# Sums, copies and one PSUM bank moved in a two-level seven-product kernel on one core

## The chip, the cores and the metric

The kernel runs on one core of one Trainium2 chip. Times are device microseconds of that core, from runs of the whole program. A profile is one more execution, taken by the hardware profiler; the span in it runs from the first to the last instruction.

The engines are named as the profile names them: PE (matmul; PEld is its weight load), DVE (vector), ACT (scalar), POOL (GpSimd), and SP, which here only issues DMAs. Each takes its instructions in the order in which the program lists them.

## What is computed

A conditioned block over x of 32 sequences x 128 tokens x 512 features, all in float32. Cut to what matters:

```python
emb = silu(t) @ ada_w + ada_b                       # shift, scale, gate per sequence
norm = where(m, layernorm(x) * (1 + scale) + shift, 0)
fwd = gelu(norm @ ssm_w1 + b1) @ ssm_w2 + b2        # bwd: the same with other weights
x = x + gate * where(m, fwd + bwd, 0)
ff_ada = silu(t) @ ffada_w + ffada_b
ff_norm = layernorm(x) * (1 + scale_mlp) + shift_mlp
h = gelu_tanh(ff_norm @ ff_w1 + ff_b1)              # 512 -> 1024
out = x + gate_mlp * (h @ ff_w2 + ff_b2)            # 1024 -> 512
```

The first half touches masked tokens only (the mask marks the tails of the sequences), the second half touches all 4096 tokens.

## The kernel before

**First half, to about 88 us.** Masked tokens are gathered into 512 slots, four tiles of 128 (s0 to s3). For each pair of tiles `hidden` (L182) forms gelu(xT w1) and `project` (L196) multiplies it with w2 into one PSUM bank `po`; bias, gate and x are then added on DVE and the rows stored to a DRAM tile, `x1_rows`. For the last tile, s3, these three steps are `with_bias`, `with_gate` and `with_x` (L1173 to L1182), and `with_x(3)` is also what issues the last store of `x1_rows`, on SP's queue. Between the matmuls of s3's `project` four transposes make xT of the second group of sequences.

**Second half.** The 32 sequences are done in four pairs of groups (`p` = 0 to 3, eight sequences a pair, four a group). A pair goes through two products:

*FirstProduct* (h = gelu(x w1)). The blocks of x and of w1 are multiplied with a scheme of seven products in place of eight, on two levels. The outer level gives seven *streams*, done in the order 1, 2, 5, 6, 3, 7, 4 (`STREAMS`); inside a stream the inner level gives seven *products*, P1 to P7. One product of one stream is a *phase* (`phase`, L896): two matmul instructions of 128x256 float32, four records in the trace. In what follows P6(1) is product P6 of stream 1. A stream has two PSUM accumulators, `e` (from the pool ps_h) and `a` (from ps_o), three buffers each in turn. Around the phases stand the sums that make the scheme work:

- `TokenBlocks.one(j)` (L767), on DVE: the *inner* sums of x that streams 1 and 2 use (s1, s2, a21, s4); 128x1024 each. P5 reads s1, P6 reads s2, P3 reads s4.
- `token_sums(j, n)` (L824), on DVE: the *outer* sums, for streams 5, 6 (tiles sx and sy), 3 and 4 (in place), each in four parts n = 0 to 3; 128x512, the last part 128x256. Part 0 serves P5 and P6, part 1 P1 and P2, part 2 P7 and P4, part 3 P3.
- `seed(j)` (L945): puts a stream's `a` (for streams with a prior result, plus that result) into `e` before P2 adds onto it. On ACT for stream 1, on DVE for the others.
- After P6 DVE writes e = a + p5 (L930), on which P3 then adds; after P7 and P4 DVE writes a sum of `a` out of PSUM (L935, L940); P2 and P3 are copied out or put through gelu by ACT. `with_p5` (L953) adds a kept P5 to a result on POOL; the sum after P6(2) reads such a result.

Streams overlap by *windows* (L994): P5, P1 of the new stream, P3, P7 of the old one, P2, P6 of the new, P4 of the old. A dictionary `fills`, filled with `put(window, place, function)`, says what else is recorded behind which phase: token sums, the gathers that overwrite masked tokens of the next pair with rows of `x1_rows` (`take_first_half`, on POOL's queue), and layernorm statistics.

*SecondProduct* (out = h w2). One level of the same scheme: P1 to P7, each for two halves of the tokens, U and V, 14 steps (`ORDER`) of eight matmul instructions. `first_block` and `second_block` (L1036, L1046) make its sums s1 and, in place, s2 on DVE; `keep_and_seed` (L795) copies `e` to a tile p5 and `a` to `e`, on ACT. P5V reads the second half of s1, which is made of gelus of the end of the first product (quarter "21" of stream 4).

The first three steps of the second product stand between the last phases of the first one (L1288 to L1307), and the next pair's stream 1 between its last steps (L1341 to L1352). For the next pair, x is normalised and transposed in 32x32 blocks on DVE, turned by 28 small DMAs on SP's queue and 4 on ACT's, and scaled on ACT.

Everything is recorded under a manual schedule: on each engine the instructions run in the order in which these functions are called. So the order of the calls is the order of the work. The SP queue at the opening of pair 0 holds, in this order: two loads of weight sums (tw, 896 KB each, `load_weights`), the store of `with_x(3)`, four loads of the next pair's x (512 KB each), and much later the next weight sums.

Of the kernel before, what the change touches and what calls it, by code (L numbers as in the profile page):

```python
# [9 lines left out]
F32 = mybir.dt.float32  # L10
# [12 lines left out]
def kernel(  # L23
# [51 lines left out]
    P = 128  # L75
# [21 lines left out]
    ps_h = ctx.enter_context(tc.tile_pool(name="ps_h", bufs=3, space=bass.MemoryType.PSUM))  # L97
    ps_o = ctx.enter_context(tc.tile_pool(name="ps_o", bufs=3, space=bass.MemoryType.PSUM))
# [45 lines left out]
    w2 = ssm.tile([P, HC, D], F32, name="w2")  # L144
# [48 lines left out]
            h.append(t)  # L193
        return h

    def project(i, h, w, name, between=None):  # L196

        po = ps_o.tile([P, 512], F32, tag="o", name=f"po_{name}_{i}")
        for f in range(HC):
            if between and f in between:  # L200
                between[f]()
            nc.tensor.matmul(po, h[f][:, ts(i, P)], w[:, f, :], start=(f == 0), stop=(f == HC - 1))  # L202
        return po
# [272 lines left out]
    for key, vec in (("ssm1", ssm_b1), ("bwd1", bwd_b1), ("ff1", ff_b1)):  # L476
        n = vec.shape[0] // P
# [133 lines left out]
    h1 = []  # L611
# [46 lines left out]
    of_x = {}  # L658
# [133 lines left out]
    def bank_of(product, unit):  # L792
        return unit[1] if product in ("P1", "P6", "P7", "P4") else unit[0]

    def keep_and_seed(unit, name):  # L795

        e, a = unit
        p5 = gp.tile([P, 512], F32, tag="p5", name=f"p5_{name}", bufs=3)
        nc.scalar.copy(p5, e)
        nc.scalar.copy(e, a)  # L800
        return p5
# [211 lines left out]
    class SecondProduct:  # L1013
# [29 lines left out]
                ALU.add,  # L1043
            )

        def second_block(self, c):  # L1046

            nc.vector.tensor_tensor(
                self.s1[c], self.s1[c], self.ha[:, : HC // 2, self.cols[c]], ALU.subtract
            )  # L1050
# [22 lines left out]
        def step(self, step, late=False):  # L1073
            p, ha, hb, s1, w = self.p, self.ha, self.hb, self.s1, fw2_of.of
            hh = HC // 2
            product, n = ORDER[step][:2], ORDER[step][2]
            c = "UV".index(n)
            tok = self.cols[c]
            e, a = self.banks[c]
            bank = bank_of(product, (e, a))  # L1080
            src = {
                "P1": ha[:, :hh, tok], "P2": ha[:, hh:, tok], "P3": ha[:, hh:, tok],
                "P4": hb[:, hh:, tok], "P5": s1[c], "P6": s1[c], "P7": hb[:, :hh, tok],
            }[product]
            last = p == NP - 1 and step == len(ORDER) - 1
            for i in range(2):
                part = bank[:, ts(i, D // 2)]
                if last:
                    part = ps_t.tile([P, 512], F32, tag="tr", name=f"last_{i}")[:, : D // 2]
                for k in range(hh):  # L1090
                    nc.tensor.matmul(  # L1091
                        part,
                        src[:, k, ts(i, P)],
                        w[product][:, k, :],
                        start=(last and k == 0),
                        stop=True,
                        skip_group_check=True,
                    )
                if last:

                    t = tp.tile([P, D // 2], F32, tag="t", name=f"t_last_{i}")
                    gate = self.gate[1][:, 2 * c + i, : D // 2]
                    nc.vector.tensor_tensor(t, part, gate, ALU.mult)
                    xt = self.xs[1][c][:, i, : D // 2]
                    nc.vector.tensor_tensor(xt, xt, t, ALU.add)
                    nc.sync.dma_start(out[(2 * p + 1) * G + 2 * c + i, :, : D // 2], xt)
            if product == "P5":
                self.p5[c] = keep_and_seed((e, a), f"o{p}_{c}")
                if not late:
                    self.second_block(c)  # L1110
            elif product == "P2":
                self.finish(c, 0, 0, e)

                nc.vector.tensor_tensor(ha[:, hh:, tok], ha[:, hh:, tok], s1[c], ALU.subtract)
            elif product == "P6":
                nc.vector.tensor_tensor(e, a, self.p5[c], ALU.add)
            elif product == "P3":
                self.finish(c, 0, 1, e)
                self.store(c, 0)
            elif product == "P7":  # L1120
                t = tp.tile([P, 512], F32, tag="t", name=f"c22_o{p}_{c}")
                nc.vector.tensor_tensor(t, a, self.p5[c], ALU.add)
                self.finish(c, 1, 1, t)
                if p == NP - 1 and n == "V":
                    b = (2 * p + 1) * G + 2 * c
                    nc.sync.dma_start(
                        out[b : b + 2, :, D // 2 :].rearrange("b s d -> s b d"),
                        self.xs[1][c][:, :, D // 2 :],
                    )
                    self.finish(c, 1, 0, a)  # L1130
            elif product == "P4" and not last:
                self.finish(c, 1, 0, a)
                self.store(c, 1)
# [20 lines left out]
    h1 = hidden(xT_t, NH, w1, 0, AF.Gelu, "s1", ssm)  # L1154
# [13 lines left out]
    def turn(k):  # L1168
        return lambda: transposed(1, xn_b, xT[1], k)
# [10 lines left out]
    def with_x(at):  # L1180
        nc.vector.tensor_tensor(tail[at], tail[at], xc[at], ALU.add)
        nc.sync.dma_start(x1_rows[ts(at, P), :], tail[at])  # L1182
# [3 lines left out]
    def keep_and_turn():  # L1186
# [2 lines left out]
        with_gate(2, gs[0])  # L1189
        with_x(2)  # L1190

    po = project(1, h1, w2, "s3", {0: turn(0), 1: turn(1), 2: keep_and_turn, 4: turn(3)})

    store_weight_sums(4, 2)
    of_x[0] = TokenBlocks(0, xT)
# [6 lines left out]
    now = FirstProduct(0, of_x[0].cut(), of_w)  # L1202
    for j in (1, 2):
        now.load_weights(j)
    now.apart(1)
    for j in (2, 3, 4):
        of_x[0].one(j)
    now.do(1, "P1")
    now.seed(1)
    now.do(2, "P1")  # L1210
    now.do(1, "P2", "P5", "P6")
    with_x(3)
    x_of[1] = load_x(1, spare)
    now.token_sums(1, 0)
    now.do(2, "P5")
    now.do(1, "P7")
    now.with_p5(2, "22")
    now.seed(2)
    now.token_sums(1, 1)
    now.do(1, "P3")  # L1220
    now.with_p5(2, "12")
# [8 lines left out]
    for p in range(NP):  # L1230
# [4 lines left out]
        def put(w, n, f, *args):  # L1235
            fills.setdefault(w, {}).setdefault(n, []).append(lambda: f(*args))

        if p:
            put(1, 1, now.token_sums, 2, 2)
            put(1, 3, now.token_sums, 2, 3)  # L1240
        for n, at in enumerate(((1, 4), (1, 6), (1, 6), (2, 1)) if p else ((2, 1), (2, 1), (2, 3), (2, 3))):
            put(*at, now.token_sums, 3, n)
        for n, at in enumerate(((2, 3), (2, 4), (2, 6), (2, 6)) if p else ((2, 4), (2, 4), (2, 6), (2, 6))):
            put(*at, now.token_sums, 4, n)
        put(3, 6, now.load_weights, 3)
        put(4, 6, now.load_weights, 4)
        second = SecondProduct(p, now.h, xs)
# [56 lines left out]
            to_feature_rows(0, nc.sync)  # L1304
        second.load_gate(1)
        second.first_block(1, 0, 2)
        second.second_block(0)  # L1307
        fill = {5: [lambda: second.third_block(0)], 7: [lambda: second.third_block(1)]}

        def put(step, f, *args):  # L1310
# [5 lines left out]
        if more_pairs:  # L1316

            for i in range(G):
                put(2 + i // 2, blocks, 1, i)
            for k in range(KC):  # L1320
                put(4 + k // 2, lambda k: scaled(2 * (p + 1), xT[0], k), k)
                put(7 + k // 2, lambda k: scaled(2 * (p + 1) + 1, xT[1], k), k)
                if k == 1:
                    put(4, to_feature_rows, 1, nc.sync, nc.sync, nc.sync, nc.scalar)

            def begin(j):
                if j == 1:
                    of_x[p + 1] = TokenBlocks(p + 1, (xT[0], xT[1]))
                of_x[p + 1].one(j)

            put(8, begin, 1)
            put(9, begin, 2)
            put(9, begin, 3)
            put(10, begin, 4)

            def next_product():
                nxt["p"] = FirstProduct(p + 1, of_x[p + 1].cut(), of_w)
                nxt["p"].load_weights(1)

            nxt = {}  # L1340
            put(10, next_product)  # L1341
            put(11, lambda: nxt["p"].do(1, "P5", "P1"))
            for n in range(4):
                put(11 + n // 2, lambda n: nxt["p"].token_sums(1, n), n)
            for n in range(2):
                put(13, lambda n: nxt["p"].token_sums(2, n), n)
            if p + 2 < NP:
                x_of[p + 2] = [[], []]
                put(11, lambda: x_of[p + 2][0].extend(load_side(p + 2, 0)))
                put(13, lambda: x_of[p + 2][1].extend(load_side(p + 2, 1)))  # L1350
            put(12, lambda: nxt["p"].do(1, "P2", "P6"))
            put(13, lambda: nxt["p"].load_weights(2))  # L1352
# [4 lines left out]
        if more_pairs:  # L1357
            now = nxt["p"]
# [11 lines left out]
    with tc.If(more > 0):  # L1370
# [11 lines left out]
        with tc.For_i(0, more, 1):  # L1382
# [12 lines left out]
            for half_no, (mod, was, wbs, bias, bcol, func) in enumerate(  # L1395
# [7 lines left out]
                for j, w in enumerate(was):  # L1403
                    n = FF // len(was)
                    nc.sync.dma_start(wa[:, :, ts(j, n)], w.rearrange("(k p) f -> p k f", p=P))
                for j, w in enumerate(wbs):
                    n = HC // len(wbs)
# [69 lines left out]
```

## Time and profile before

| | us |
|---|---|
| median of 3 runs | 466.88 |
| the runs | 464.16, 466.93, 466.88 |
| the profiled execution | 463.4 |
| its span | 461.7 |

The granted clock of PE was 0.998 of full speed over the span. By stretches of the span (busy us of each engine, then the mean busy share of the DMA engines):

| stretch, us | what runs | PE | DVE | ACT | POOL | DMA |
|---|---|---|---|---|---|---|
| 0 to 58 | first half, slots 0 to 255 | 51.90 | 37.91 | 11.61 | 11.86 | 0.95 |
| 58 to 88 | first half, slots 256 to 511 | 30.00 | 24.54 | 11.06 | 13.23 | 0.43 |
| 88 to 111 | pair 0, first product, opening | 21.84 | 22.83 | 11.08 | 10.51 | 0.74 |
| 111 to 144 | pair 0, first product, rest | 32.94 | 24.09 | 17.19 | 25.61 | 0.31 |
| 144 to 175 | pair 0, second product | 30.90 | 21.83 | 13.79 | 0.00 | 0.53 |
| 175 to 199 | change to pair 1 | 23.47 | 22.95 | 7.71 | 7.52 | 0.68 |
| 199 to 267 | pair 1 | 67.84 | 48.36 | 33.29 | 28.17 | 0.40 |
| 267 to 358 | pair 2 | 90.84 | 68.60 | 41.02 | 36.15 | 0.48 |
| 358 to 462 | pair 3 | 98.91 | 61.03 | 28.48 | 24.79 | 0.26 |

How to read it: a busy PE is not PE at its peak, since ends of matmuls are modelled; whether PE lost time is seen from the distance between starts. Two instructions of an engine can overlap by some hundredths of a us in a timeline, for the same reason. A timeline merges like instructions that follow each other (x2 is two), and gives the idle time ahead of one only from 0.15 us or so on. The name of a tile leaves its buffer's number out, so that `e_m` is the accumulator e of any stream.

### The profile page before, as it was taken

To read this page: it belongs to the slowest core of one execution; us is meant where nothing else is said; L and a number is where in the kernel's file an instruction comes from. 1 tells how busy PE (TensorE), PEld (TensorE's weight loads), DVE (VectorE), ACT (ScalarE), POOL (GpSimd) and SP (SyncE) were. 2 spreads that over 40 slices of the span, in tenths; PEclk is the share of its full clock that TensorE was granted. 3 is DMA by queue.
4 is the path that set the end of the run, shared out by engine and by line. 5 is a ranking of instruction groups with operands and counts; after the bars stand their busy time and mean duration, and the time that the engine had idled before them with its cause. 6 is when DMAs were issued, how large, how long until landed. Compare 5 with 4: busy or idle time off the path is not lost.

```text
span 461.7 us, 5825 instructions
## 1 busy us (share of the span) xinstructions
PE 448.6 (97%) x2000; PEld 364.2 (79%) x2000; DVE 332.1 (72%) x538; ACT 175.2 (38%) x380; POOL 157.8 (34%) x153
## 2 busy tenths in 40 slices
PE   6899999999999999999999999999999999999995
PEld 2385385677888888788888888888888888888884
DVE  4649868999678839986787498867873995434645
ACT  3121021744445361344455513444455144562000
POOL 6210083048980000489700005987000025660000
PEclk9999999999999999999999999999999999999999
DMA  8999835692207734833077258220872342222022
GB/s 276 386 407 361 307 136 88 204 346 88 106 5 224 105 84 137 297 100 130 1 229 114 69 182 298 92 87 14 226 108 67 134 163 79 81 85 98 0 85 101
DMA packets 82418, 70.41 MB, mean 153 GB/s; under 512 B 63168, under 2 KB 63696, under 8 KB 81362
## 3 DMA queue, kind: packets, MB, share of 16 engines
q1 hardware_dynamic: 67298, 57.03, 39.4%
q0 software_dynamic: 4480, 11.66, 7.1%
q10 hardware_dynamic: 10608, 1.32, 2.0%
q8 instruction: 17, 0.28, 0.2%
q14 instruction: 15, 0.12, 0.1%
HBM read 56.83 MB, written 13.17 MB: 152 GB/s over the span
## 4 chain that ended last, share of the span: by engine, by line
PE 69%; DVE 9%; ACT 7%; POOL 5%; SPq 4%; issue 4%; DMA 1%; POOLq 0%; ACTq 0%; DVEq 0%
PE a_m L905 15%; PE a_o L1091 14%; PE e_m L905 12%; PE e_o L1091 12%; PE ph_s L188 6%; PE po_s L202 4%; SPq L744 4%; POOL hb L989 2%; ACT hb L867 2%; ACT xT L727 1%; DVE sx L834 1%; DVE xT L725 1%; ACT ha L867 1%; DVE xn_sy L838 1%; PE part_s L282 1%
## 5 line engine op out<-in xcount | busy, mean ns | idle before, releaser
L956 POOL TENSOR_TENSOR ha<-p_m,ha 128x512 f32<-128x512 f32 x20 | 26.9, 1345 | 152.5 <-ACT ha L963 143.3
L1091 PE MATMUL e_o<-fw,ha 128*128 128x256 f32 x256 | 57.9, 379 | 0.0
L727 ACT ACTIVATE xT<-xT,modT 128x128 f32<-128x128 f32 x112 | 44.1, 480 | 30.5 <-DMA xT<-xn 30.3
L1091 PE MATMUL a_o<-t,hb 128*128 128x256 f32 x240 | 54.1, 379 | 0.0
L1091 PEld LDWEIGHTS e_o<-fw,ha 128*128 128x128 f32 x256 | 48.6, 190 | 6.6
L1091 PEld LDWEIGHTS a_o<-t,hb 128*128 128x128 f32 x240 | 45.6, 190 | 6.2
L673 POOL DMA_INDIRECT x<-x_rows,slot_i x32 | 36.4, 1136 | 28.7 <-DMA x_rows<-t_s 18.1
L867 ACT ACTIVATE hb<-hb,biasT 128x256 f32<-128x256 f32 x64 | 29.0, 501 | 27.8 <-POOL hb L989 19.3
L956 POOL TENSOR_TENSOR hb<-p_m,hb 128x512 f32<-128x512 f32 x20 | 28.2, 1409 | 20.4 <-DVE hb L935 20.1
L919 ACT COPY p_m<-e_m 128x512 f32<-128x512 f32 x27 | 15.8, 585 | 49.2 <-PE e_m L905 46.8
L1091 PE MATMUL e_o<-fw,s 128*128 128x256 f32 x128 | 29.2, 381 | 0.5 <-DVE s L1039 0.3
L963 ACT COPY ha<-e_m 128x512 f32<-128x512 f32 x32 | 18.5, 578 | 28.0 <-PE e_m L905 27.7
L1091 PE MATMUL a_o<-t,s 128*128 128x256 f32 x128 | 28.9, 379 | 0.0
L1091 PE MATMUL a_o<-fw,ha 128*128 128x256 f32 x128 | 28.9, 379 | 0.0
L202 PE MATMUL po_s<-w,h_s 128*128 128x512 f32 x64 | 28.6, 593 | 0.0
L188 PE MATMUL ph_s<-xT_s,w 128*128 128x256 f32 x128 | 28.6, 382 | 0.0
L1091 PEld LDWEIGHTS e_o<-fw,s 128*128 128x128 f32 x128 | 24.1, 190 | 4.8 <-DVE s L1039 1.7
L188 PEld LDWEIGHTS ph_s<-xT_s,w 128*128 128x128 f32 x128 | 24.0, 190 | 4.7 <-ACT h_s L192 1.5
L1091 PEld LDWEIGHTS a_o<-t,s 128*128 128x128 f32 x128 | 24.3, 190 | 3.3
L1091 PEld LDWEIGHTS a_o<-fw,ha 128*128 128x128 f32 x128 | 24.3, 190 | 3.3
L867 ACT ACTIVATE ha<-e_m,biasT 128x256 f32<-128x256 f32 x48 | 20.0, 468 | 15.5 <-PE e_m L905 10.2
L930 DVE TENSOR_TENSOR e_m<-a_m,ha 128x512 f32<-128x512 f32 x20 | 13.9, 697 | 16.6 <-POOL ha L956 6.6
(210 smaller groups left out, 870.3 us busy)
## 6 DMA issues: line engine op xcount, KB each, us to landing
tw<-t_rows SPq DMA_DIRECT2D x16, 896.0 KB, 4.7
x<-in_x_dram SPq DMA_DIRECT2D x16, 512.0 KB, 8.4
gate<-gate_rows POOLq DMA_DIRECT2D x8, 1024.0 KB
out_dram<-x SPq DMA_DIRECT2D x15, 512.0 KB, 3.1
xT<-xn SPq DMA_DIRECT2D x92, 64.0 KB, 2.4
fw<-in_L_cond_ff_w_dram SPq DMA_DIRECT2D x2, 2048.0 KB
ada_f<-in_L_cond_ffada_w_dram SPq DMA_DIRECT2D x4, 768.0 KB, 13.7
ada_a<-in_L_cond_ada_w_dram SPq DMA_DIRECT2D x4, 512.0 KB, 5.9
```

What stands on the lines that cost most here:

```text
L188: nc.tensor.matmul(ph[:, :n], w[:, k, ts(f, P)], xT[:, k, :], start=(k == 0), stop=(k == KC - 1))
L202: nc.tensor.matmul(po, h[f][:, ts(i, P)], w[:, f, :], start=(f == 0), stop=(f == HC - 1))
L673: nc.gpsimd.indirect_dma_start(out=xs[i // G][i % G // 2][:, i % 2], out_offset=None, in_=x1_rows[:slots, :], in_offset=bass.IndirectOffse ...
L727: nc.scalar.activation(out, src, AF.Identity, bias=shift, scale=scale)
L744: queues[b % len(queues)].dma_start(dst[ts(q, R), b], src[ts(b, R), q])
L867: nc.scalar.activation(dst[:, n], src[:, n], AF.Gelu_apprx_tanh, bias=biasT[:, f : f + 1])
L905: nc.tensor.matmul(bank[:, ts(n, QT)], self.w_block(j, product)[:, ts(n, P)], self.x_block(j, product), start=(product in ("P1", "P5") and ...
L919: nc.scalar.copy(p5, e)
L930: nc.vector.tensor_tensor(e, a, p5, add)
L956: nc.gpsimd.tensor_tensor(self.place(RESULT[j], c), self.p5[j], other, ALU.add)
L963: nc.scalar.copy(self.place(RESULT[j], c), src)
L1091: nc.tensor.matmul(part, src[:, k, ts(i, P)], w[product][:, k, :], start=(last and k == 0), stop=True, skip_group_check=True,)
```

## The change

Nothing is computed otherwise; the same instructions run, with the same sizes. What moves:

1. *Bank.* `project` can be told from which PSUM pool its bank comes; the last tile, s3, takes one of ps_h in place of ps_o.
2. *Opening of pair 0, on DVE.* Before: s2, a21, s4, then the sum after P6(1), `with_x(3)`, sx part 0, the sum after P7(1), the seed of stream 2, sx parts 1 to 3, the sum after P6(2). After: s2, a21, the sum after P6(1), s4, the seed of stream 2, the sum after P7(1), sx part 0, `with_x(3)`, sx parts 1 to 3, the sum after P6(2). PE's order is as it was. The order on POOL and SP is as it was too, but the store of `with_x(3)` and the x loads behind it on SP follow a DVE instruction that now stands later.
3. *Windows of pairs 1 to 3, on DVE.* Before: sy parts 0 and 1, the seed of stream 2, sy part 2, the sum after P7(1), sy part 3, the first part of stream 3's sum, the sum after P6(2), then the other parts. After: sy part 0, the seed of stream 2, the sum after P7(1), sy parts 1 and 2, the sum after P6(2), sy part 3 and stream 3's sum, whose last part stands behind the sum after P7(2).
4. *Second product, on ACT.* `keep_and_seed` of the first half (U) is called with the second block and no more right behind P5U. On ACT the order was: gelus of the end of stream 4 (two), copy to p5, copy to e, gelus (two); it becomes four gelus, then the two copies. This holds in every pair.

```diff
-    def project(i, h, w, name, between=None):
+    def project(i, h, w, name, between=None, bank=(ps_o, "o")):
-        po = ps_o.tile([P, 512], F32, tag="o", name=f"po_{name}_{i}")
+        pool, tag = bank
+        po = pool.tile([P, 512], F32, tag=tag, name=f"po_{name}_{i}")
...
-        def second_block(self, c):
+        def seed_and_second_block(self, c):
+            self.p5[c] = keep_and_seed(self.banks[c], f"o{self.p}_{c}")
             nc.vector.tensor_tensor(
                 self.s1[c], self.s1[c], self.ha[:, : HC // 2, self.cols[c]], ALU.subtract
             )
...
             if product == "P5":
-                self.p5[c] = keep_and_seed((e, a), f"o{p}_{c}")
                 if not late:
-                    self.second_block(c)
+                    self.seed_and_second_block(c)
...
-    po = project(1, h1, w2, "s3", {0: turn(0), 1: turn(1), 2: keep_and_turn, 4: turn(3)})
+    between = {0: turn(0), 1: turn(1), 2: keep_and_turn, 4: turn(3)}
+    po = project(1, h1, w2, "s3", between, (ps_h, "h"))
...
-    for j in (2, 3, 4):
+    for j in (2, 3):
         of_x[0].one(j)
     now.do(1, "P1")
     now.seed(1)
     now.do(2, "P1")
     now.do(1, "P2", "P5", "P6")
+    of_x[0].one(4)
+    now.do(2, "P5")
+    now.seed(2)
+    now.do(1, "P7")
+    now.with_p5(2, "22")
+    now.token_sums(1, 0)
     with_x(3)
     x_of[1] = load_x(1, spare)
-    now.token_sums(1, 0)
-    now.do(2, "P5")
-    now.do(1, "P7")
-    now.with_p5(2, "22")
-    now.seed(2)
     now.token_sums(1, 1)
     now.do(1, "P3")
     now.with_p5(2, "12")
...
         if p:
-            put(1, 1, now.token_sums, 2, 2)
-            put(1, 3, now.token_sums, 2, 3)
-        for n, at in enumerate(((1, 4), (1, 6), (1, 6), (2, 1)) if p else ((2, 1), (2, 1), (2, 3), (2, 3))):
+            for n, at in enumerate(((1, 3), (1, 4), (1, 6))):
+                put(*at, now.token_sums, 2, 1 + n)
+        for n, at in enumerate(((1, 6), (2, 1), (2, 1), (2, 3)) if p else ((2, 1), (2, 1), (2, 3), (2, 3))):
             put(*at, now.token_sums, 3, n)
-        for n, at in enumerate(((2, 3), (2, 4), (2, 6), (2, 6)) if p else ((2, 4), (2, 4), (2, 6), (2, 6))):
+        for n, at in enumerate(((2, 4), (2, 4), (2, 6), (2, 6))):
             put(*at, now.token_sums, 4, n)
...
         second.first_block(1, 0, 2)
-        second.second_block(0)
+        second.seed_and_second_block(0)
...
-            for n in range(2):
-                put(13, lambda n: nxt["p"].token_sums(2, n), n)
+            put(13, lambda: nxt["p"].token_sums(2, 0))
```

## The prediction

> **What bounds the kernel now.** I read the page's busy shares and chain first, then the timelines of PE, DVE, POOL and ACT around the three places that the change touches. Columns of a timeline: start and length in us, engine, line, operation, tiles, then in brackets the idle time before it and what ended it. The page:
>
> ```profile
> PE 448.6 (97%) x2000; PEld 364.2 (79%) x2000; DVE 332.1 (72%) x538; ACT 175.2 (38%) x380; POOL 157.8 (34%) x153
> PE 69%; DVE 9%; ACT 7%; POOL 5%; SPq 4%; issue 4%; DMA 1%; POOLq 0%; ACTq 0%; DVEq 0%
> ```
>
> PE carries the chain. One phase (four matmul records) starts 0.86 us after the last when nothing is missing; anything over that is lost. The opening of pair 0, PE:
>
> ```profile
> 87.96 1.03 PE L905 MATMUL a_m_alone<-xT,fw 128*128 128x256 f32 x4
> 89.12 1.10 PE L905 MATMUL a_m<-xT,fw 128*128 128x256 f32 x4
> ...
> 93.84 1.13 PE L905 MATMUL a_m_alone<-xT,t 128*128 128x256 f32 x4 [0.17 <-DVE e_m L930]
> ...
> 96.36 1.13 PE L905 MATMUL e_m<-xT,fw 128*128 128x256 f32 x4 [0.53 <-DVE e_m L949]
> ...
> 104.59 1.13 PE L905 MATMUL a_m<-xT,t 128*128 128x256 f32 x4 [0.19 <-DVE hb L935]
> ```
>
> Start to start, with about 0.1 for the slower first matmuls behind a stop, I count losses of 0.37 (89.12), 0.43, 0.79, 0.45, then 0.15 and 0.40 at 107.33 and 109.47, and 0.27 each at 120.10 and 122.11. In later pairs: 0.42 at each of 144.10, 236.50 and 327.80; 0.48, 0.37 and 0.44 at 189.47, 191.57 and 198.98; 0.10, 0.08 and 0.20 at 281.54, 306 and 372.90. From 58 us to the end PE loses 6.2 us in all: no edit here can give more.
>
> But who is late? DVE and POOL at the opening:
>
> ```profile
> 91.96 1.22 DVE L774 TENSOR_TENSOR s<-xT,s 128x1024 f32<-128x1024 f32 x1
> 93.09 0.69 DVE L930 TENSOR_TENSOR e_m<-a_m_alone,p_m 128x512 f32<-128x512 f32 x1
> 93.69 0.68 DVE L1181 TENSOR_TENSOR t_s<-t_s,xc 128x512 f32<-128x512 f32 x1
> ...
> 95.62 0.69 DVE L949 TENSOR_TENSOR e_m<-a_m,ha 128x512 f32<-128x512 f32 x1
> 96.21 2.36 DVE L834 TENSOR_TENSOR sx<-xT 128x512 f32<-128x512 f32 x2
> 98.50 1.49 DVE L834 TENSOR_TENSOR sx<-s 128x256 f32<-128x256 f32 x1
> 99.91 0.69 DVE L930 TENSOR_TENSOR e_m<-a_m,ha 128x512 f32<-128x512 f32 x1
> ```
>
> ```profile
> 96.29 1.73 POOL L956 TENSOR_TENSOR hb<-p_m,hb 128x512 f32<-128x512 f32 x1 [18.78 <-DVE hb L935]
> 97.99 1.72 POOL L956 TENSOR_TENSOR ha<-p_m,ha 128x512 f32<-128x512 f32 x1
> 102.35 1.37 POOL L673 DMA_INDIRECT x<-x_rows,slot_i  x1 [2.65 <-DMA x<-in_x_dram]
> ```
>
> No DVE line from 80 to 113 us shows idle time: the opening is bound by DVE's total, not by its order. POOL has no gap from 102.35 to 127, and the waits of 120.10 and 122.11 hang on it (DVE's sum at 119.35 had waited 2.02 us for POOL). The end of the first product, ACT:
>
> ```profile
> 141.34 0.57 ACT L799 COPY p_o<-e_o 128x512 f32<-128x512 f32 x1
> 141.93 0.57 ACT L800 COPY e_o<-a_o 128x512 f32<-128x512 f32 x1
> 142.42 0.91 ACT L867 ACTIVATE hb<-hb,biasT 128x256 f32<-128x256 f32 x2
> ```
>
> **What the Trainium skill says.** "PSUM — Partial Sum Buffer", section "PSUM bank collisions raise a hardware error": accesses are guarded by bank. The trace agrees: a_m of stream 2, in po_s3's buffer, starts at 89.12 only when the bias add of 88.29 (0.68) has read it. Section "Engine vs sequencer instructions": the ACT, DVE and GpSimd queues are strict FIFO, so order alone can cost. "SBUF — State Buffer", section "Who interferes with whom": a DVE instruction with two SBUF inputs and a GpSimd one that reads SBUF lock each other out. The trace agrees: the two POOL adds take 1.73 and 1.72 us here against 1.27 at 121.94, and the DVE sums beside them (2.36 for two, 1.49 for a half one) against 0.68 and 0.41.
>
> **The change, part by part.** Units: DVE 128x512 sum 0.60 start to start, 128x1024 1.13; PE phase start to its reader 1.06 (P7(1) 93.84, less its 0.1, to DVE 95.01); DVE start to the PE phase behind it 0.75 (93.09 to 93.84).
>
> *Bank.* Stream 2's first phase no longer waits: P6(1) starts 91.41 instead of 91.78. The ring of ps_h shifts by one; its buffers' last readers were gelus before 73 us, so no new wait.
>
> *Opening order.* DVE comes to the P6(1) sum at 91.96 but PE gives it at 91.41 + 1.06 = 92.47: DVE now idles 0.51. Then sum 92.47, s4 93.07, seed 94.20, P7(1) sum 94.80, sx0 95.40, with_x, sx1 to sx3. P7(1) starts 93.22, P3(1) waits for s4 to 94.35 (before 94.81), P2(2) 95.3 (before 96.36): the 0.43 and 0.79 go. But the next sum, P6(2), stands behind the same set of DVE work. Four sums, a half one, and the two POOL adds that lock DVE for about 1.19 each: 95.40 + 2.74 + 2.38 = 100.5; before, 99.91. P3(2) needs it: about 101.2 against 100.78. So PE ends the reordering about 0.5 late; 0.54 of it is swallowed by the POOL waits at 120.10 and 122.11. Net 0 (ends: −0.4 if the locks fall on sums from PSUM, +0.8).
>
> *SP and POOL behind it.* with_x goes from 93.69 to about 97.2, its store from 94.40 to 97.9, and with it four x loads that stand behind on SP. The first gather waits for the first load's landing: 101.50 in the trace. There the loads queued behind weight loads (those end at 98.5); issued 3.5 later they find idle DMA engines: store 97.9, load 98.3, plus about 3.5 (a lone 256 KB store took 2.0; 256 packets of 2 KB pass in 1.35), so 101.9. POOL starts 0.4 late (ends 0 and 3.5) and, having no slack, hands it on: **+0.4** for pair 0.
>
> *Window order, pairs 1 to 3.* Moving one 0.60 sum (and its lock) behind the seed and the P7(1) sum frees 0.48 and 0.37 at 189 to 192, 0.10 at 281, 0.20 at 372. In pair 1 it meets the next thing: P5(6) at 198.98 starts right behind tw's last packet (198.47), whose load SP issues behind the last store and x loads. That does not move, so pair 1 gives 0; pairs 2 and 3 give **−0.3**. Sums of streams 3 and 4 shift by some slots inside windows 1 and 2 where DVE idles 0.63 at 196.29: 0 (ends −0.2, +0.5).
>
> *ACT copies.* The last two gelus can start when DVE's P4 sum is done, 140.79 + 0.65, near 141.5 instead of 142.42; DVE's s1 sum then follows its transpose, 142.56 instead of 143.35, and P5V is ready at 143.3, before its turn at 143.79. The copies, now 142.4 to 143.6, feed P2U at 147.66: covered by 3.5 us of P5V. Gone: 0.42 in pairs 0, 1 and 2. Pair 0's is hidden again: pair 1 starts on xT, whose DMAs SP issues without a break from 143.13 to 163.9, whatever PE does. Left: **−0.85** (ends 0, −1.3).
>
> Sum: 0.4 − 0.3 − 0.85 = **−0.75 us**, span 461.7 to about 460.95. The profiled execution took 463.4, 3.5 under the median of 466.88; the same step from the median is 466.1.
>
> **Rivals.** *All stops go*: if DVE kept up, everything named up to 122 except the POOL waits, the 0.48, 0.37, 0.10, 0.20, and three times 0.42: 2.6 + 1.15 + 1.26, near −4.5 with side effects, 462.4. Against it: DVE's unbroken row. *Slower*: the x loads land the full 3.5 later; POOL's chain, hence PE at 120.10, moves 3.5; +3.5 − 1.15 = +2.35, 469.2. It decides once the first gather starts later than 103.5 (102.35 + 1.15). For it: POOL waited on just this load, 2.65. Against it: the loads were held by other traffic. *Nothing shows*: DVE or DMA hides pairs 2 and 3 as well; 0, 466.9.
>
> **Numbers.** Chances: forecast 0.5, all stops 0.12, slower 0.2, nothing 0.18. A change under 1% cannot be told from none here; the three runs alone spread 0.6%. Forecast 466.1; range 463.0 to 468.2, from half of the full gain with the spread of the runs to most of the slower case. Over 1% faster needs 4.7 of the 6.2 us lost: 0.05, over 1% slower 0.03, within 1% 0.92.
>
> **What would show it.** Right: a_m of stream 2 0.86 behind the phase before; a DVE gap of 0.5 before the P6(1) sum; P3(2) no earlier than 100.7; first gather at 102.3 to 103.2; no stop at 236 and 328, but one before P5(6) of pair 1. Wrong: P3(2) near 99.7 (order counted after all), or a gather past 103.5.

## The result, and the profile after

| | before | after |
|---|---|---|
| median, us | 465.41 (21 runs, 463.07 to 467.85) | 465.20 (21 runs, 462.27 to 468.52) |
| the profiled execution | 463.4, span 461.7 | 462.27, span 460.6 |

The ratio of after to before is 1.0003, 95% interval 0.9986 to 1.0020: no change that can be measured. The two traces differ by 1.1 us, but the execution profiled of the changed kernel was the shortest of its 21 and that of the kernel before lay 2.0 under its median. So traces are used below for where a wait is, and timings for what it is worth.

The page of the changed kernel, busy shares and chain by engine:

```profile
PE 447.5 (97%) x2000; PEld 364.8 (79%) x2000; DVE 331.0 (72%) x538; ACT 175.4 (38%) x380; POOL 157.5 (34%) x153
PE 74%; DVE 10%; SPq 4%; DMA 3%; issue 3%; ACT 3%; POOL 2%; ACTq 0%; DVEq 0%; POOLq 0%
```

Busy times are the same within 0.3%. The chain lost ACT and POOL (12% before, 5% now) and gained PE and DMA (1% before, 3% now): a transfer has become a wait. From 58 us on PE loses 5.4 us of starts, 6.2 before. PE's timeline of the opening (L906 is L905 of before; lines move by one to three):

```profile
87.81 1.03 PE L906 MATMUL a_m_alone<-xT,fw 128*128 128x256 f32 x4
88.67 1.03 PE L906 MATMUL a_m<-xT,fw 128*128 128x256 f32 x4
89.80 1.13 PE L906 MATMUL e_m<-xT,fw 128*128 128x256 f32 x4
...
101.32 0.92 PE L906 MATMUL e_m<-s,fw 128*128 128x256 f32 x3 [1.24 <-DVE e_m L931]
```

P1(2) follows P1(1) after 0.86: the wait for the bank is gone. But P2(1) follows only after 1.13, and its first matmul is slow. ACT's timeline says why:

```profile
83.00 6.26 ACT L728 ACTIVATE xT<-xT,modT 128x128 f32<-128x128 f32 x16 [0.27 <-DMA xT<-xn]
89.17 0.58 ACT L952 COPY e_m<-a_m_alone 128x512 f32<-128x512 f32 x1
```

The copy that seeds `e` of stream 1 stands behind sixteen scalings of xT; P2(1) needs it. The 0.37 of the bank, with 0.1 for slow first matmuls in it, came back here. DVE's timeline, same stretch:

```profile
92.75 0.70 DVE L931 TENSOR_TENSOR e_m<-a_m_alone,p_m 128x512 f32<-128x512 f32 x1 [0.86 <-ACT p_m L920]
...
96.29 0.69 DVE L1182 TENSOR_TENSOR t_s<-t_s,xc 128x512 f32<-128x512 f32 x1
96.89 3.44 DVE L835 TENSOR_TENSOR sx<-xT 128x512 f32<-128x512 f32 x2
...
100.58 0.68 DVE L931 TENSOR_TENSOR e_m<-a_m,ha 128x512 f32<-128x512 f32 x1
```

DVE, which had no gap before, now idles 0.86 ahead of the sum after P6(1), and with_x(3) (L1182) has moved from 93.69 to 96.29. Two sums that take 0.60 each alone took 3.44: POOL's two additions ran beside them. POOL's timeline:

```profile
96.36 1.74 POOL L957 TENSOR_TENSOR hb<-p_m,hb 128x512 f32<-128x512 f32 x1 [18.91 <-DVE hb L936]
98.07 1.71 POOL L957 TENSOR_TENSOR ha<-p_m,ha 128x512 f32<-128x512 f32 x1
103.23 1.17 POOL L674 DMA_INDIRECT x<-x_rows,slot_i  x1 [3.45 <-DMA x<-in_x_dram]
```

POOL's first gather waits 3.45 for the x load that stands behind with_x(3), and starts at 103.23 (before 102.35).

Later, all three stops before P5V are gone, and those before P2(2) of pairs 1 to 3 too. In their place PE stops before P5(6) of pair 1 and of pair 2. First the kernel before, in pair 1, then the changed one:

```profile
198.98 1.10 PE L905 MATMUL e_m<-xn_sy,tw 128*128 128x256 f32 x4 [0.21 <-issue]
...
198.68 1.10 PE L906 MATMUL e_m<-xn_sy,tw 128*128 128x256 f32 x4 [0.52 <-DMA tw<-t_rows]
...
289.62 1.10 PE L906 MATMUL e_m<-xn_sy,tw 128*128 128x256 f32 x4
```

Counted as in the prediction, 0.75 is lost in pair 1 (0.44 before) and 0.30 in pair 2 (0.10 at the P2(2) of pair 2 before); pair 3 has 0.23 at 398.64, before P5(4). tw's last packets end at 198.15, 289.14 and 398.07, about half a us ahead of each of these starts: PE has caught up with its weight sums.

### The profile page after: what moved, and what is told of

It reads as the page before. It is cut to its first block, busy times and chain, and to the rows that moved or that the text cites. A ratio compares the mean times of both kernels' runs of the same rounds, so it can differ in the third digit from the quotient of the medians.

```text
span 460.6 us, 5827 instructions
## 1 busy us (share of the span) xinstructions
PE 447.5 (97%) x2000; PEld 364.8 (79%) x2000; DVE 331.0 (72%) x538; ACT 175.4 (38%) x380; POOL 157.5 (34%) x153
## 4 chain that ended last, share of the span: by engine, by line
PE 74%; DVE 10%; SPq 4%; DMA 3%; issue 3%; ACT 3%; POOL 2%; ACTq 0%; DVEq 0%; POOLq 0%
PE a_o L1093 17%; PE a_m L906 16%; PE e_o L1093 13%; PE e_m L906 12%; PE ph_s L188 6%; PE po_s L203 4%; SPq L745 4%; DMA tw<-t_rows 2%; ACT xT L728 1%; DVE sx L835 1%; DVE xT L726 1%; DVE s L775 1%; PE part_s L283 1%; PE pm_f L263 1%; PE last L1093 1%
```

## The experiments

All ratios are to the kernel before, with the 95% interval. The last two columns are from each kernel's trace, in us behind its own P1(1): the start of P3(2), and of P3(3).

| label | what | median | ratio | P3(2) | P3(3) |
|---|---|---|---|---|---|
| (before) | | 465.41 | 1 | 12.83 | 32.15 |
| (after) | parts 1 to 4 | 465.20 | 1.0003 (0.9986 to 1.0020) | 13.51 | 32.97 |
| x1_copies | before, part 4 | 464.97 | 1.0000 (0.9969 to 1.0030) | 12.83 | 33.42 |
| x2_windows | before, part 3 | 464.60 | 0.9979 (0.9962 to 0.9996) | 12.83 | 33.77 |
| x3_opening | before, parts 1 and 2 | 466.77 | 1.0033 (1.0012 to 1.0054) | 13.57 | 33.03 |
| x4_early_x | after, with_x(3) early | 463.97 | 0.9977 (0.9954 to 0.9999) | 13.28 | 32.73 |
| x5_p5_on_dve | after, two additions to DVE | 465.87 | 1.0007 (0.9990 to 1.0025) | 12.67 | 35.10 |
| x6_tw_first | after, tw ahead of x | 462.91 | 0.9959 (0.9943 to 0.9976) | 13.27 | 32.72 |
| x8_p5_first | after, P5(1) ahead of P2(1) | 462.13 (1 run) | | 13.15 | 32.61 |
| x7_best | x5, x6, x8, with_x(3) early | 463.46 | 0.9967 (0.9951 to 0.9982) | 11.76 | 34.18 |
| x9_gathers | x7, three gathers later | 462.66 | 0.9948 (0.9927 to 0.9969) | 11.75 | 32.87 |
| x10_gathers_alone | after, three gathers later | 466.03 | 1.0010 (0.9991 to 1.0029) | 13.50 | 35.04 |
| x11_gathers_pool | x9 without x5's edit | 463.20 | 0.9968 (0.9947 to 0.9990) | 12.90 | 32.70 |
| x12_old_opening | before, parts 3 and 4, tw ahead of x | 463.23 | 0.9941 (0.9917 to 0.9966) | 12.83 | 33.76 |

### The parts alone

The first four test the theory that the change is a sum of a loss in the opening and gains later, against the rival that each part is hidden by itself. The diffs of x1, x2 and x3 are the hunks of their parts in the change. x4 puts with_x(3) and the x loads directly behind the sum after P6(1):

```diff
     now.do(1, "P2", "P5", "P6")
+    with_x(3)
+    x_of[1] = load_x(1, spare)
     of_x[0].one(4)
...
-    with_x(3)
-    x_of[1] = load_x(1, spare)
     now.token_sums(1, 1)
```

x1_copies:

> The kernel before with part 4 alone (copies behind the gelus). Theory (each part is hidden in part by what is late next): the stops of about 0.42 us before P5V are gone in pairs 0, 1 and 2; pair 0's gain comes back as a longer stop at P2(2) or P4(1) of pair 1, where DVE and the turning DMAs set the time, so the stops at 189 to 192 grow from 0.85 to about 1.25; span about 0.85 shorter than before (461.7 to 460.9), ratio about 0.998. Rival (all of it reaches the end): 1.26 shorter, and no stop grows. Rival (nothing): the stops move behind another ACT wait, span unchanged.

No stop before P5V is left. In pair 3 the stop before P2(2) grew from 0.20 to 0.84. In pair 1 it grew from 0.48 to 0.89, but the 0.37 before P4(1) went, so the two together came to 0.89 and not to the 1.25 expected, and the stop before P5(6) shrank from 0.44 to 0.07. So this trace shows the theory's longer stop in pair 3 only. The timing shows nothing, in an interval of 0.3% either way.

x2_windows:

> The kernel before with part 3 alone (windows of pairs 1 to 3). Theory: the stops at P2(2) and P4(1) are gone in pairs 1 to 3 (0.85, 0.10, 0.20), but the stop before P5(6) grows in pair 1 from 0.44 to about 1.3, because the load of weight sums lands when it did; 0.3 at most is left from pairs 2 and 3; ratio 0.999 to 1.000. Rival (order counts in full): P5(6) of pair 1 starts 0.85 earlier, span about 1.15 shorter, ratio 0.9975.

The stops at P2(2) and P4(1) of pairs 1 to 3 are gone, and P5(6) of pair 1 stopped for 1.78, longer than the theory's 1.3. The timing is 0.21% better, as the rival had it, and more than that trace lets one see. One reading is that parts 3 and 4 open each other's way: P5V early is worth something only where P2(2) does not wait, and both end at tw. That is not tested; no run has these two parts alone.

x3_opening:

> The kernel before with parts 1 and 2 alone (bank and opening). Theory (DVE's total binds, and the x loads come late): P3(2) starts about 0.5 later than before (near 101.3) behind one stop of about 1.5 us, the first gather starts near 103.2 instead of 102.35, and PE leaves the stops at 120 to 122 about 0.7 to 0.8 later than before; span 0.5 to 0.8 longer unless pair 1 hides it, ratio 1.001 to 1.002. Rival (PE's order counts): the opening ends at least 0.5 earlier, ratio below 0.999.

The timing puts the cost of the opening by itself at 0.33%, some 1.5 us, with 0.12% to 0.54% in the interval. The trace repeats the marks of the changed kernel, with P2(1) late by 0.42 and P3(2) by 1.51, but does not show where 1.5 us would be lost. Its first gather came at 102.35, no later than before, but took longer with those behind it, and P3(3), at 33.03, lies among the starts that kernels with the old opening have (32.15 to 33.77).

x4_early_x:

> The changed kernel with with_x(3) and the x loads right behind the P6(1) sum, as early as before; all else as changed. Theory (POOL's chain from the first gather sets pair 0): DVE's total is the same, so P3(2) still starts near 101.3 with its stop of about 1.5, but the first gather starts near 102.3 instead of 103.2, and the stop before P3(3) near 120 ends about 0.8 earlier than in the changed kernel; span about 0.7 shorter than the changed kernel's, near 459.9. Rival (DVE's lateness of 0.5 alone made pair 0 late): the first gather comes earlier but PE at P3(3) stays where it is in the changed kernel.

The ratio is 0.9977 against 1.0003 for the changed kernel, with intervals that overlap. The first gather started 14.23 behind P1(1), not 15.42, but P3(3) came only 0.24 earlier, at 32.73 in place of the 0.8 expected. x6 below, which leaves with_x(3) late, has it at 32.72. So it is not shown that the place of with_x(3) carries the opening's cost.

### Who holds PE up to 120 us

x5 takes POOL's two additions off the sums of sx, x8 the copy on ACT off P2(1):

```diff
-            nc.gpsimd.tensor_tensor(self.place(RESULT[j], c), self.p5[j], other, ALU.add)
+            engine = nc.vector if (self.p, j) == (0, 2) else nc.gpsimd
+            engine.tensor_tensor(self.place(RESULT[j], c), self.p5[j], other, ALU.add)
```

```diff
-    now.do(1, "P2", "P5", "P6")
+    now.do(1, "P5", "P2", "P6")
```

x8_p5_first:

> The changed kernel with P5(1) ahead of P2(1) on PE in the opening. Theory (P2(1) waits for the copy of a to e on ACT, which stands behind ACT's scalings of xT, and this ate the gain of the bank): the stop of 0.36 before P2(1) goes, P6(1) starts 3.44 us behind P1(1) in place of 3.82, the sum after P6(1) comes about 0.4 earlier on DVE, and P3(2) about 0.4 earlier, near 13.1 behind P1(1). Rival (PE is slow there for a reason of its own): P6(1) stays at 3.8. The time moves by less than 0.5 us in either case, since POOL sets P3(3).

PE's timeline of it:

```profile
88.80 1.03 PE L906 MATMUL a_m<-xT,fw 128*128 128x256 f32 x4
89.67 1.03 PE L906 MATMUL e_m_alone<-s,fw 128*128 128x256 f32 x4
90.53 1.03 PE L906 MATMUL e_m<-xT,fw 128*128 128x256 f32 x4
91.39 1.03 PE L906 MATMUL a_m_alone<-s,t 128*128 128x256 f32 x4
```

P6(1) (the last line) now starts 3.45 behind P1(1) (87.94), in place of 3.82, and every phase 0.86 behind the one before: the seed copy did eat the bank's gain. (In x4 and x6 the copy happened to start 1.12 behind P1(1), not 1.36, and P6(1) came at 3.58.) P3(2) came 0.36 earlier, at 13.15.

x5_p5_on_dve:

> The changed kernel with the two additions of kept P5 to stream 2 in pair 0 on DVE in place of POOL. Theory (DVE and POOL shut each other out in the opening, at about 1.19 us an addition): DVE gains two sums of 0.60 and loses two locks of 1.19, so P3(2) starts about 12.3 us behind P1(1), in place of 13.51; the two sums of sx that took 1.76 each take 0.68. Rival (no lock, the long sums are slow for a reason of their own): DVE only gains work, P3(2) about 14.7 behind P1(1). In the time both expect little: POOL's six gathers start where they did (first gather 15.4 behind P1(1), since with_x(3) stands where it stood), and P3(3) stays near 33 behind P1(1); ratio to the kernel before 0.999 to 1.002.

The sums of sx took 0.69 each, and P3(2) came 0.84 earlier with more work on DVE. The lock is real, and smaller than the 1.19 expected. But P3(3) came 2.13 later. DVE and POOL of that kernel, from the timeline of all engines:

```profile
104.98 2.33 POOL L674 DMA_INDIRECT x<-x_rows,slot_i  x1 [0.30 <-issue]
...
106.34 0.70 DVE L931 TENSOR_TENSOR e_m<-a_m,p_m 128x512 f32<-128x512 f32 x1
...
107.61 1.83 POOL L674 DMA_INDIRECT x<-x_rows,slot_i  x1 [0.30 <-issue]
...
108.47 0.70 DVE L950 TENSOR_TENSOR e_m<-a_m,ha 128x512 f32<-128x512 f32 x1
```

A gather takes 1.00 on POOL when nothing disturbs it; these took 2.33 and 1.83. Each began inside a run of DVE sums that read two SBUF tiles, and each ended 0.97 after that run did: at 107.31, where DVE's first sum with a PSUM input began at 106.34, and at 109.44, against 108.47. The Trainium skill, "SBUF — State Buffer", section "SBUF: two separate sides", says that a DMA issued from GpSimd's queue has its descriptors written by GpSimd, which can't do so while DVE runs an operation in a two-port mode. DVE's instructions here are sums of two tensors, which the same page, in "Who interferes with whom", says were not seen to stall a DMA. These traces differ from that. After 80 us the fourteen traces hold 336 gathers. The 162 that began while no DVE sum of two SBUF tiles was running took 0.99 to 1.12; the 174 that began beside one took 0.99 to 2.43, and all twelve that took more than 1.8 ended 0.95 to 0.98 after the run of sums. So gathers are held up beside such sums; which step of a gather is held is not shown. Not every gather is caught: 27 of the 174 took no more than 1.01, as did the changed kernel's third, at 106.00, which began 0.06 ahead of the next sum of a run. What lets one pass stays open.

Why this decides is seen in all traces together. Behind P1(1), in us:

| | first gather | the six gathers take | POOL's first addition of stream 6 | P3(3) | difference |
|---|---|---|---|---|---|
| before | 14.40 | 6.76 | 22.71 | 32.15 | 9.44 |
| x1_copies | 14.72 | 7.74 | 24.01 | 33.42 | 9.41 |
| x2_windows | 14.24 | 8.55 | 24.34 | 33.77 | 9.43 |
| x12_old_opening | 13.87 | 8.93 | 24.34 | 33.76 | 9.42 |
| after | 15.42 | 6.56 | 23.53 | 32.97 | 9.44 |
| x3_opening | 14.59 | 7.45 | 23.59 | 33.03 | 9.45 |
| x4_early_x | 14.23 | 7.52 | 23.30 | 32.73 | 9.44 |
| x6_tw_first | 15.21 | 6.53 | 23.29 | 32.72 | 9.43 |
| x8_p5_first | 15.05 | 6.57 | 23.17 | 32.61 | 9.43 |
| x5_p5_on_dve | 15.80 | 8.32 | 25.67 | 35.10 | 9.44 |
| x7_best | 15.29 | 7.92 | 24.75 | 34.18 | 9.44 |

P3(3) starts 9.41 to 9.45 behind the first addition of stream 6 in every kernel that keeps POOL's order, wherever P3(2) stood (11.76 to 13.57). So the opening's end is set by when the x load lands and by how long six gathers take: DVE's order and the bank count only through these two. The first four kernels have one opening, and their gathers took 6.76 to 8.93: the trace that the prediction was made on had the shortest. With the new order of DVE and with_x(3) late (after, x3, x5, x6, x8 and x10) the first gather starts 14.59 to 15.80 behind P1(1), with the old one 13.87 to 14.72.

### Moving the gathers

x9 and x10 move three gathers of pair 0, x11 is x9 with the additions of stream 2 back on POOL:

```diff
-            put(2, 6, take_first_half, p + 1, x_next, range(G, G + 2))
-            put(3, 4, take_first_half, p + 1, x_next, range(G + 2, G + 3))
+            put(*((2, 6) if p else (3, 4)), take_first_half, p + 1, x_next, range(G, G + 2))
+            put(*((3, 4) if p else (4, 4)), take_first_half, p + 1, x_next, range(G + 2, G + 3))
```

x10_gathers_alone:

> The changed kernel with the same move of three gathers and nothing else. Theory: stream 6's additions start near 108.6 in place of 111.34, and the stops of 0.27 before P3(3) and P2(7) go; P3(2) stays at 13.5 behind P1(1); about 0.5 us, ratio to the kernel before 0.998 to 1.000. Rival (those stops hang on DVE's own sums as well): P3(3) stays within 0.2 of 32.97 behind P1(1), ratio as that of the changed kernel, 1.000 to 1.001.

The additions came early, 20.52 behind P1(1), and P3(3) came late, 35.04: neither theory. From the timeline of all engines:

```profile
109.36 1.28 POOL L957 TENSOR_TENSOR ha<-p_m,ha 128x512 f32<-128x512 f32 x1
109.49 2.93 DVE L845 TENSOR_TENSOR xT<-xT,xn_sy 128x512 f32<-128x512 f32 x1
...
110.59 1.27 POOL L957 TENSOR_TENSOR hb<-p_m,hb 128x512 f32<-128x512 f32 x1
112.34 0.41 DVE L845 TENSOR_TENSOR s<-s,xn_sy 128x256 f32<-128x256 f32 x1
```

Here POOL holds DVE: two additions back to back, and a DVE sum of two SBUF tiles that waits through both of them (2.93 for 0.60). PE stopped 2.66 at 113.42 for the sum behind it. In the changed kernel those additions ran from 111.34 on, beside DVE work that reads PSUM or one tile, and neither was slowed.

x9_gathers:

> The version of all favoured edits (label x7_best) with pair 0's fifth and sixth gather moved from in front of stream 6's additions on POOL to behind them, and the seventh from in front of stream 3's additions to behind them. Theory (what DVE gains in the opening is handed back because POOL's gathers take 1.0 to 2.4 us beside DVE's sums and stand ahead of the additions that P6(6), P3(6), P3(3) wait for): stream 6's additions start near 109.5 in place of 112.33, the stops of 1.82, 0.62, 0.50 and 0.17 between 114 and 124 shrink to less than 0.4 together, P3(3) starts about 31.3 behind P1(1), P5V of pair 0 about 55.0; some 2.5 us less than x7_best (0.9967), ratio to the kernel before 0.991 to 0.994. Rival (the gathered rows come too late for the statistics on DVE, or pair 1 opens on its x loads anyway): P3(3) comes early but P2(2) or P5(6) of pair 1 stop for more than 1 us, ratio 0.995 to 0.998.

x11_gathers_pool:

> The version x9_gathers with stream 2's two additions of kept P5 in pair 0 back on POOL, as in both kernels. Theory (beside them each DVE sum of two SBUF inputs is held for about 1.1 us): P3(2) about 12.8 to 13.2 behind P1(1) in place of 11.8, and about 1 us more in all than x9_gathers: ratio to the kernel before 0.993 to 0.996. Rival (once POOL's additions come early, the opening is bound elsewhere): ratio within 0.001 of x9_gathers.

In x9 the stops of x7 at 114 to 118 went, and one of 1.91 before P3(3) came: two gathers now stood in front of stream 3's additions in place of one, and P3(3) moved to 10.74 behind stream 6's first addition, 1.30 more, which is a gather of 1.00 with its 0.30 ahead. Three of the four gathers in front were slowed (1.55, 2.33, 1.83). Another stop, of 0.95 at 128.58, looks like x10's: a DVE instruction on four columns of SBUF (0.85 in the changed kernel) came later than there, met two POOL additions, and took 2.48, with the sum that PE waited for behind it. DVE and POOL of x9:

```profile
125.44 2.48 DVE L711 TENSOR_SCALAR ve<-mv 128x4 f32<-128x4 f32 x1
...
125.40 1.26 POOL L958 TENSOR_TENSOR hb<-p_m,hb 128x512 f32<-128x512 f32 x1
126.62 1.26 POOL L991 TENSOR_TENSOR ha<-ha 128x512 f32<-128x512 f32 x1
```

x9's ratio lies between the ranges of its theory and its rival, and its P3(3), at 32.87, is not the 31.3 of the theory. In x11 P3(2) came at 12.90, as expected, but the ratio is neither in the theory's range nor within 0.001 of x9. x9 was 0.19% better than x7, x11 0.20% behind x9, both within the intervals.

### tw ahead of the x loads

```diff
-                put(13, lambda: x_of[p + 2][1].extend(load_side(p + 2, 1)))
             put(12, lambda: nxt["p"].do(1, "P2", "P6"))
             put(13, lambda: nxt["p"].load_weights(2))
+            if p + 2 < NP:
+                put(13, lambda: x_of[p + 2][1].extend(load_side(p + 2, 1)))
```

x6_tw_first:

> The changed kernel with one SP order swapped: in step 13 of the second product the load of the next weight sums (tw of stream 6) stands ahead of the loads of the x of the pair after next. Theory (P5(6) waits for tw because SP issues it behind the x loads): the stops before P5(6) of pair 1 (0.75) and pair 2 (0.30) go, about 1.0 us; ratio 0.002 below that of the changed kernel (1.0003), about 0.998. The 0.23 before P5(4) of pair 3, where no x is loaded, stays. Rival (the transfer itself is limited by the other traffic, or the next wait takes over): the stops move by less than 0.2 or another appears before P3(6), and the ratio stays within 0.001 of the changed kernel's.

PE's timeline of pair 1, P5(6) on the second line:

```profile
197.78 1.03 PE L906 MATMUL a_m<-xT,t 128*128 128x256 f32 x4
198.64 1.03 PE L906 MATMUL e_m<-xn_sy,tw 128*128 128x256 f32 x4
```

0.86 apart: no stop, nor in pair 2. tw's last packets end at 195.38 here, in place of 198.15. The swap has this effect in all five traces that have it: in x6, x7, x9, x11 and x12 these packets end at 194.21 to 197.67, without the swap at 198.15 to 202.00. None of the five stops at tw, while of the nine without it eight stop before P5(6) of pair 1, for 0.44 to 1.78, and x1 for 0.07. The 0.23 of pair 3, which was to stay, did not show; it is missing in some traces without the swap too (x4, x8). In x6 a stop of 0.28 before P2(2) of pair 1 came instead. From the start of P5V of pair 0 to that of the last group of matmuls it is 306.85 us, 307.77 in the changed kernel and 309.20 before: 0.92 of the 1.0 expected. The ratio, 0.9959, is 0.44% under the changed kernel's, more than the trace accounts for; the intervals leave 0.1% to 0.8%. It is faster than both kernels. The swap was run only on top of other parts of the change, not on the kernel before alone.

x7_best:

> All that the runs so far favour, together: the changed kernel with tw ahead of the x loads in step 13, the two additions of kept P5 in pair 0 on DVE, P5(1) ahead of P2(1), and with_x(3) with its store and the x loads in the place where DVE idles ahead of the sum after P6(1). Theory: P6(1) 3.4 behind P1(1), P3(2) 11 to 12, first gather 13.7 to 14.5, P3(3) 31.5 to 33, no stop before P5V, before P2(2) in pairs 1 to 3 and before P5(6); ratio to the kernel before 0.994 to 0.997, some 2 us less. Rival (gains of different places hide each other behind POOL's gathers and the x loads of the next pair): ratio 0.998 to 1.000, with stops before P3(3) or P5(6) that grow by what was gained ahead of them.

The ratio lies in the theory's range. P3(2) starts without a stop at last, but P3(3) comes later than in the changed kernel, at 34.18 and not at 31.5 to 33: stops such as the rival named, before P3(6), P2(3) and P3(3) (1.92, 0.72, 0.60), took back the opening, while the later pairs kept their gains.

x12_old_opening:

> The kernel before with the window order (part 3), the copies behind the activations (part 4) and tw ahead of the x loads in step 13; bank and opening of pair 0 (parts 1 and 2) as in the kernel before. Theory (the new opening costs about what label x3_opening measured alone, 0.33%, and the other parts keep their gains): the stops before P5V, before P2(2) of pairs 1 to 3 and before P5(6) are gone as in x6_tw_first, and the ratio to the kernel before lies below that of x6_tw_first (0.9959), at 0.992 to 0.9945. Rival (the opening's cost is not additive: with either opening POOL's gathers beside DVE's sums set P3(3), and the old opening meets slower gathers as often): ratio 0.995 to 0.997, P3(3) more than 33 behind P1(1).

0.9941 lies in the theory's range, and P3(3), at 33.76, is what the rival named. Against x6_tw_first it is 0.18% less, with intervals that overlap for the most part. x12, x9 and x6 cannot be told apart; each is faster than before. Whether the new opening costs anything of its own is not settled: the timing of x3 says 0.33%, but the traces with the old opening have P3(3) at 32.15 to 33.77 and those with the new one, otherwise untouched, at 32.72 to 33.03.

## Why the prediction was right, and which of its terms were not

The forecast, a gain below what can be told from none, held: 465.20 lies in the range of 463.0 to 468.2. That says little for the sum behind it. The range is 5.2 us wide and holds the rival of no gain (466.9) too, and its base, the median of three runs, was 1.5 above that of the 21. -0.75 us is a ratio of 0.9984, just under the interval's lower end of 0.9986, while no change at all lies inside: the gain was rather smaller than forecast, and in the time the rival "Nothing shows" fits better. In part the forecast was lucky, as its steps show:

- *Bank.* P1(2) 0.86 behind P1(1), as said. That P6(1) would start 0.37 earlier was wrong: 3.82 behind P1(1) in both traces. The step looked at what P1(2) waited for and not at what P2(1) would wait for next, a copy on ACT behind the scalings of xT; x8 showed it, a cost of ACT's order alone.
- *Opening order.* DVE's gap before the sum after P6(1) came (0.86, said 0.5), and P3(2) came at 101.32 (said about 101.2), but through two errors that cancel. The sum after P6(1) started at 92.75 and not 92.47, since the bank's gain did not come. And each addition on POOL held DVE for 1.08, not 1.19: in the prediction's own lines 96.21 to 99.91 is 3.70, for two sums and a half that take 1.54 alone, and in the changed kernel two sums take 3.36 in place of 1.20. That there is a lock at all was shown by x5. "Net 0" for PE was right for the reason given, that POOL's waits swallow it; they swallow anything up to there.
- *SP and POOL behind it.* The path, from the load over POOL's gathers to P3(3), was right, the term +0.4 mis-sized. The load was issued at 97.38 and landed at 102.38, 5.0 us later, not 3.5. The sum assumed that the DMA engines would be idle by then, but they were not: their mean busy share was 0.77 from 97.4 to 98.4, and the last packets of the weight sums ended at 99.14 (in the kernel before at 99.2, where the prediction read 98.5). In the six traces with this order (after, x3, x5, x6, x8, x10) the load took 4.12 to 5.04; what sets that, and what the other three x loads add, is not shown. The first gather started 15.42 behind P1(1) against 14.40, +1.02; the six gathers together were 0.20 quicker; P3(3) moved +0.82. But the base was a trace whose gathers were the shortest of four with that opening. Against the other three (33.42 to 33.77) the changed kernel's P3(3), at 32.97, is early, so that even the sign of this term is open: the lengths of the gathers alone spread by more than 2 us (6.76 to 8.93), and one trace of each kernel can't give it.
- *Window order.* Pair 1: the stops of 0.48 and 0.37 went and the one before P5(6) grew, as said, but by 0.31 and not by all of it. Pairs 2 and 3: 0.10 and 0.20 went, and 0.30 and 0.23 came at tw. That tw would be late next was foreseen for pair 1 alone. x6 showed it for pairs 1 and 2; the stop of pair 3 comes and goes from trace to trace. So do those at P2(2): other traces with the new order have up to 0.42 there in pair 1 (x4, x9) and up to 0.44 in pair 3 (x11).
- *ACT copies.* All three stops of 0.42 before P5V went, as said. That -0.85 of it reaches the end is not shown: x1, with these copies alone, came to 1.0000, in an interval from 0.9969 to 1.0030 that holds the term and holds nothing.
- *Rivals.* "All stops go" was excluded by DVE as argued, and by POOL, which the text had named for two stops only and which bounds all that comes before them. "Slower" had its first gather at 103.5 or later; it came at 103.23, and the loss grows with POOL's delay from the first tenth on, so the point "from which it decides" measured only where the loss outweighs the other gains. "Nothing shows" had as its reason that pairs 2 and 3 are hidden too, and there the traces agree with it: what P2(2) no longer waits for comes back at tw.

## What to carry to other kernels

Before counting what a reordering frees, follow the engine that stands between it and the end, and check with one subtraction over several traces: where a later instruction keeps the same distance to a queue's step in all of them, that queue sets it, and gains ahead of it are lost. When a stop goes, look up the transfer that lands next after it: here one swapped load, made on top of the change, was worth more than the whole change (0.9959 against 1.0003). Where DVE and GpSimd both run on SBUF tiles, what they do at the same moment is part of the cost, and moving either moves it.

## What the runs showed of the hardware

After 80 us an indirect gather on POOL took from 0.99 to 2.43 us, and the lengths come in recurring sets (2.43 then 1.83; 1.50, 1.23, 1.50), as the gathers fall against DVE's sums. No gather there that began clear of DVE's sums with two SBUF inputs took more than 1.12, and the twelve that took more than 1.8 ended 0.95 to 0.98 us after a run of such sums. The Trainium skill, "SBUF — State Buffer", section "A bandwidth-pool intuition that's wrong (but worth ruling out)", describes such a DMA, beside a DVE tensor_copy, as blocked until shortly after DVE's end. In the changed kernel's first half a gather of 1.39 us, begun at 67.95 beside a DVE tensor_scalar, ended 1.00 after it. The times above show the like beside sums of two tensors, though not for every gather, and a gather's own time of about 1 us follows the block. In the other direction each of two POOL additions held DVE's sums for 1.08 us in the opening, and in x10 one DVE sum of 0.60 took 2.93 beside two of them.
